# Head of a four-layer graph kernel: unread matmuls while x loads, the first tile by quarters, other orders for the first tiles

## The chip, the cores and the metric

The kernel runs on one core of a Trainium2 chip. The metric is the device time of one execution in microseconds; lower is better. The engines are named as in the profile: PE does matrix products, DVE, ACT and POOL work on vectors, SP issues DMAs.

## What is computed

x has 128 graphs of 64 nodes with 256 features, in float32. Four layers, each with a LayerNorm (without scale) and a ReLU ahead of it, add their result to x. Only the first half of layer 0 is touched here:

```python
h = jnp.maximum(_layernorm(x, axis=-1), 0.0)
h = relu(einsum('ts,bsh->bth', adj, h @ Wg0 + bg0))
h = relu(einsum('ts,bsh->bth', adj, h @ Wg1 + bg1))
# then four LSTMs over windows of 1 to 4 nodes, and x = x + h
# layer 1: graph convolution with two batchnorms; layer 2: three-part graph
# convolution; layer 3: attention within each graph with adj as an added mask
```

## The kernel before, in words

x is seen as 8192 rows of 256 and cut into 16 tiles of 512 rows (`SUP`), each of four quarters (`Q`) of 128 rows: two graphs side by side, so that one 128x128 matrix with adj twice on its diagonal (`adjT_bd`) aggregates both. Tiles are numbered from 0 here.

`graph_part(s)` (from line 427 on) lists the steps of tile s. Each step is put into a list by `at(t, fn, ...)` with a due time, counted from 10 x s (`ROUND`); at the end all steps of all tiles are sorted by due time and called in that order. Nothing else sets the order: each engine executes its instructions in the order in which they were called, and waits on semaphores for what they need. The due times are numbers written by hand, not measured times. The steps of one tile:

- `load` (433): a DMA for x, for tiles 0 and 1 one for each quarter. For tile 0, two quarters are issued by ACT and two by SP.
- `stats` (445): for a quarter, L446 and L447 on DVE, mean and variance.
- `root` (449): L451 on DVE adds eps, L452 on POOL raises to the power -0.5, for several quarters at once.
- `shift` (454): L455 on DVE, minus mean over deviation. `relu` (458): L459 on ACT, one a quarter.
- `aggregate0` (461): L467 on PE, for each half c of the features four 128x128 products of a quarter with `adjT_bd`, into one PSUM bank. `aggregated` (470): L471 on ACT copies the bank to SBUF.
- `weigh` (473): L477 on PE, times Wg0, four 128x256 products for each pair of quarters; `weighed` (480): L483 on DVE adds the bias term `rsb`; `relu1` (486): L488 on ACT.
- the second aggregation, again L467 and L471, a round later.
- `sums` (494): four L498 on POOL, differences of quarters of the matrix. They belong to a product with Wg1 in seven block products instead of eight; `product` (501): L506 on PE, which also needs sums of the blocks of Wg1 (L311 on POOL, from the copies L135). `begun` (509): L513, and `add` (518): L520, on DVE, empty the PSUM banks of the products; a bank is filled by one product, emptied by L513, and filled by the next. `relu2` (535): L536 on ACT.

So a steady round of PE holds seven 128x256 products (L506) of tile s-2, eight 128x128 products (L467) for tile s and eight for tile s-1, and eight 128x256 products (L477). For each tile, DVE calls L455 of a later tile between the L520 and the L513 of an earlier one.

Beside this, POOL prepares the weights of the later LSTMs in the graph part. The constants come first: `first_constants` (adjT), wg0, `second_constants` (adj, bg0), `more_constants` (Wg1 in four copies by L135, and small ones). `row_sums` (155) makes the bias terms from adj (L157, L158) and a product with a matrix of ones (L160, copied by L161). `adjacency_parts` (191) makes four masked forms of adj on POOL (L193 to L202), which SP then stores to DRAM (L203, `parts_d`). Behind it in SP's queue stand the loads of the weights for layer 1 (`load_raw_w1`, L626, into `wc`) and for the LSTM of windows of two (`staging`, L362, into `wb`); POOL adds blocks of them (L311, L369, L384, L389) at due times set by `stage`. L632 stores the sums in `wc` to DRAM (`w_d` in the profile), and after that L369 uses `wc` for the next sums.

Buffers: x has three (`pax`), the other tiles of the graph part two, the LayerNorm's small ones three; PSUM has eight banks, given out in turn by `bank()`.

Of the kernel before, what the change touches and what calls it, by code (L numbers as in the profile page):

```python
# [9 lines left out]
F32 = mybir.dt.float32  # L10
# [4 lines left out]
P = 128  # L15
# [5 lines left out]
def kernel(ctx: ExitStack, tc: tile.TileContext, a: dict, out: bass.AP):  # L21
# [4 lines left out]
    nc = tc.nc  # L26
# [4 lines left out]
    KC = D // P  # L31
    SUP = 512
    NS = NT // SUP
    Q = SUP // P
# [27 lines left out]
    def other_end(name, bufs):  # L62
        scope = ExitStack()
        return scope, scope.enter_context(tc.tile_pool(name=name, bufs=bufs, side="right"))
# [3 lines left out]
    graph_weights, first = other_end("first", 1)  # L68
# [13 lines left out]
    def bank(pool="psum"):  # L82
        return pool() if callable(pool) else banks[pool][1].tile([P, 512], F32, tag="ps", name="ps")
# [4 lines left out]
    def load_const(name, src, shape, pool=const, queue=nc.sync):  # L88
        t = pool.tile(shape, F32, tag=name, name=name)
        queue.dma_start(t, src)  # L90
        return t
# [5 lines left out]
    def weight(name, src, pool=const, queue=nc.sync):  # L97
        k, m = src.shape
        return load_const(name, src.rearrange("(c p) m -> p c m", p=P), [P, k // P, m], pool, queue)

    ident = const.tile([P, P], F32, tag="ident", name="ident")
    make_identity(nc, ident)
    ones = first.tile([P, P], F32, tag="ones", name="ones")
    nc.gpsimd.memset(ones, 1.0)
    mhalf = const.tile([P, 8], F32, tag="mhalf", name="mhalf")
    nc.gpsimd.memset(mhalf, -0.5)
    mone = const.tile([P, Q], F32, tag="mone", name="mone")
# [4 lines left out]
    adjT_bd, adj_bd = (first.tile([P, P], F32, tag=n, name=n) for n in ("adjT_bd", "adj_bd"))  # L112
# [36 lines left out]
    rs_row = first.tile([P, P], F32, tag="rs_row", name="rs_row")  # L149
# [5 lines left out]
    def row_sums():  # L155

        nc.vector.reduce_sum(rs_col, adj_bd, axis=AX.X)  # L157
        nc.vector.tensor_scalar_mul(rsb, con["bg0"], rs_col)  # L158
        ps = bank()
        nc.tensor.matmul(ps[:, :P], ones, adjT_bd, start=True, stop=True)  # L160
        nc.vector.tensor_copy(rs_row, ps[:, :P])  # L161

    def adjacencies():

# [258 lines left out]
    ROUND, HALF = 10.0, SUP // 2  # L423
    with tc.tile_pool(name="pa", bufs=2) as pa, tc.tile_pool(name="pax", bufs=3) as pax:
        events, wih0, made = [], [], []

        def graph_part(s):
            t0, v = ROUND * s, {}

            def at(t, fn, *args):  # L430
                events.append((t0 + t, len(events), fn, args))
# [35 lines left out]
                    nc.tensor.matmul(p_[:, ts(q, P)], v[h][:, q, ts(c, P)], adjT_bd,  # L467
                                     start=True, stop=True)

            def aggregated(g, c):  # L470
                nc.scalar.copy(v[g][:, c, :], v["p", g, c])  # L471

            def weigh(k):
                p_ = v["W", k] = bank().rearrange("p (q d) -> p q d", q=2)
# [67 lines left out]
                at(-10.5, second_constants)  # L542
                at(-20, lambda: con.update(wg0=weight("wg0", a["Wg0"], first)))
            if s == 0:
                halves = ((slice(0, 2), -9.1), (slice(2, 4), -7.4))
                at(-10, new_norm)
                for q in range(Q):
                    at(-9.8 + 0.6 * q, stats, q)
            else:
                halves = ((slice(0, 4), -11.9),)  # L550
                at(-15.2, new_norm)
                for q in range(Q):
                    at((-15.1, -14.5, -13.1, -12.5)[q], stats, q)
            for qs, t in halves:
                at(t, root, qs)
                at(t + (1.4 if s < 2 else 3.0), shift, qs)
                for q in range(qs.start, qs.stop):
                    at((2.7 - ROUND if s == 1 else t + (1.5 if s == 0 else 3.1)) + 0.6 * (q - qs.start), relu, q)
            late, end = 0, s == NS - 1
            for c in range(KC):  # L560
                at(late + 0.86 + 1.75 * c, aggregate0, "g0", "h", c)
                at(late + 0.87 + 1.75 * c, aggregated, "g0", c)
            for k in range(2):
                at(late + 6.56 + 1.72 * k, weigh, k)
                at(late + 8.3 + 1.75 * k, weighed, k)
                at(late + 8.9 + 1.75 * k, relu1, k)
            late += ROUND
            for c in range(KC):
                t = (0.86, 2.6)[c] if end else 4.35 + 0.89 * c
                at(late + t, aggregate0, "g1", "h1", c)  # L570
                at(late + t + 0.01, aggregated, "g1", c)
# [19 lines left out]
            at(late + 7.1, relu2, 1)  # L591

            if s == 0:
                at(2, row_sums)
            if s == 1:
                at(-5, adjacency_parts)
            if s == 2:
# [13 lines left out]
        for s in range(NS):  # L611
            graph_part(s)
# [327 lines left out]
    def first_step(t0, st, tags, names):  # L940

        p, N = st["p"], st["N"]
        input_ = input_sums(st, 0)
        for k in (-9, -8.5, 0.2, 0.4) if st["new"] else (*((-0.8, -0.6) if p == NL else (-3.4, -1.4)), 2.6, 6.6):
            at(t0 + k, next, input_)
        g, end, t = {}, {}, t0
        for (name, gi, fn), tag in zip((g for g in GATES if g[0] != "f"), tags):
            g[name], end[name] = gate(t, st, p - 1, gi, fn, tag, names)
            t += 7
        e = end["g"]  # L950
        cell = cells[st["s"]]

        def start(n):
            i, g_ = (gates[g[k]["tag"]][:, n, :, :N] for k in "ig")
            nc.gpsimd.tensor_mul(cell[:, n, :, :N], i, g_)  # L955

        def squash(n):
            nc.scalar.activation(gates[g["g"]["tag"]][:, n, :, :N], cell[:, n, :, :N], AF.Tanh)

        h_at = t + 13.3  # L960
        for n in range(2):
            at(e + 2.2 + 0.1 * n, start, n)
            at(e + (6.07, 9)[n], squash, n)
            at(h_at + 0.8 * n, state, st, n, g["o"], g["g"], p == 1)
        st["h_at"] = h_at + 0.8
        return t
# [284 lines left out]
    t, tags = 0.0, [0, 1, 2, 3, 4]  # L1251
    plan(t, 2, (2, load_r), *((11 + 3 * k, fetch, name) for k, name in enumerate(("W1", "S1", "S2"))),
         (8, fetch_x), (20, fetch_w2), (25, fetch, "S4"), (28, fetch_s3, 0))
    for p in range(1, NL + 1):
        pairs = pairs_of(p)
        for k in range(0, len(pairs), 2):
# [3 lines left out]
            for i, st in enumerate(sts):  # L1260
                if p == 1:
                    t = first_step(t, st, [tags[(3 * (k + i) + n) % 5] for n in range(3)], FIRST_BANKS)
                else:
# [4 lines left out]
                    t = first_step(t, st, tags[:3] if i == 0 else [*tags[3:], tags[0]], GROUP_BANKS)  # L1268
# [7 lines left out]
            for j in range(1, p):  # L1276
                for st in sts:
# [5 lines left out]
                    t = outer_step(t, st, j, now, fin)  # L1283
                    tags = [now[n] for n in ("spare", "12", "22", "11", "21")]
                    now = dict(zip(("22", "11", "21", "12", "spare"), tags))
            if end and p < NL:
                q = p + 1
# [124 lines left out]
    with tc.tile_pool(name="pz", bufs=1, reuse_waits="tile") as pz:  # L1412
# [248 lines left out]
        late = ctx.enter_context(tc.tile_pool(name="late", bufs=1, side="right", reuse_waits="tile"))  # L1661
# [473 lines left out]
```

## Time and profile before

| | us |
|---|---|
| median of 4 runs (1817.31 to 1818.14) | 1817.99 |
| the profiled execution | 1818.14 |
| its span, from the first instruction to the last | 1816.40 |
| PE busy | 1793.9 (99%) |
| DVE, POOL, ACT busy | 1259.6, 1248.9, 926.9 |
| DMA packets' share of the 16 engines, first queue | 15.3% |

The profile's page gives busy times; its views answer for a stretch of the span. In the timeline each row has the start, the duration, the engine, the line, the operation, what it writes and reads, and xN where N records are merged into one row; in brackets stands the idle time of the engine just before it, with what ended it. A float32 matmul leaves two records. The waits view gives for each engine and line what it waited for: the sum, the number of times, the longest. An engine's name with a q (SPq) is its queue, which issues DMAs. The DMA view gives the time from issue to landing. DMA records and semaphore updates are in the trace too.

### The profile page before, as it was taken

To read this page: it belongs to the slowest core of one execution; us is meant where nothing else is said; L and a number is where in the kernel's file an instruction comes from. 1 tells how busy PE (TensorE), PEld (TensorE's weight loads), DVE (VectorE), ACT (ScalarE), POOL (GpSimd) and SP (SyncE) were. 2 spreads that over 40 slices of the span, in tenths; PEclk is the share of its full clock that TensorE was granted. 3 is DMA by queue.
4 is the path that set the end of the run, shared out by engine and by line. 5 is a ranking of instruction groups with operands and counts; after the bars stand their busy time and mean duration, and the time that the engine had idled before them with its cause. 6 is when DMAs were issued, how large, how long until landed. Compare 5 with 4: busy or idle time off the path is not lost.

```text
span 1816.4 us, 25209 instructions
## 1 busy us (share of the span) xinstructions
PE 1793.9 (99%) x8904; PEld 1330.5 (73%) x8904; DVE 1259.6 (69%) x2462; ACT 926.9 (51%) x1612; POOL 1248.9 (69%) x1275
## 2 busy tenths in 40 slices
PE   8999999999999999999999999999999999999998
PEld 7997444576576888788577776666444899999997
DVE  6875555676666787777677777687876666666675
ACT  6775666633534434434633333577675444444542
POOL 6988454767776777787768887777363666666663
PEclk9999999999999999999999999999999999999999
DMA  6753300000004000001200000333100110111111
GB/s 188 240 189 134 126 1 0 1 1 1 0 1 135 1 1 1 1 1 40 96 0 1 0 1 23 128 120 127 61 1 15 33 48 30 42 47 48 47 36 36
DMA packets 73868, 90.92 MB, mean 50 GB/s; under 512 B 5264, under 2 KB 64528, under 8 KB 73744
## 3 DMA queue, kind: packets, MB, share of 16 engines
q1 hardware_dynamic: 73296, 89.03, 15.3%
q8 instruction: 71, 1.16, 0.3%
q14 instruction: 53, 0.43, 0.1%
q10 hardware_dynamic: 448, 0.30, 0.1%
HBM read 56.01 MB, written 33.29 MB: 49 GB/s over the span
## 4 chain that ended last, share of the span: by engine, by line
PE 57%; DVE 1%; ACT 1%; issue 0%; POOL 0%; DVEq 0%; POOLq 0%; ACTq 0%
PE ps L1080 14%; PE ps L1846 8%; PE ps L1107 7%; PE ps L1323 5%; PE ps L1573 5%; PE ps L1813 3%; PE ps L1917 3%; PE ps L1914 3%; PE ps L908 2%; PE ps L736 2%; PE ps L1953 2%; PE ps L1984 1%; PE ps L689 1%; PE ps L1881 1%; PE ps L1757 1%; PE ps L1857 1%
## 5 line engine op out<-in xcount | busy, mean ns | idle before, releaser
L1092 DVE TENSOR_TENSOR gate<-gate,ps 128x512 f32<-128x512 f32 (+2 forms) x544 | 321.6, 602 | 165.0 <-PE ps L1080 148.4
L1126 ACT ACTIVATE gate<-gate,lbias 128x512 f32<-128x512 f32 (+2 forms) x284 | 173.2, 650 | 326.0 <-DVE gate L1120 312.1
L921 DVE TENSOR_TENSOR gate<-gate,ps 128x512 f32<-128x512 f32 (+2 forms) x162 | 100.5, 642 | 126.9 <-PE ps L908 118.8
L1140 POOL TENSOR_TENSOR cell<-cell,gate 128x1024 f32<-128x1024 f32 (+2 forms) x36 | 73.0, 2029 | 112.5 <-ACT gate L1126 112.5
L1107 PE MATMUL ps<-tx,wb 128*128 128x512 f32 (+2 forms) x320 | 143.5, 537 | 0.0
L1789 ACT ACTIVATE h<-x,ln_rn 128x256 f32<-128x256 f32 x128 | 66.5, 590 | 98.4 <-POOL ln_rn L1786 96.8
L917 ACT ACTIVATE gate<-gate,lbias 128x512 f32<-128x512 f32 (+2 forms) x108 | 95.8, 887 | 34.2 <-DVE gate L921 34.2
L908 PE MATMUL ps<-tx,wih 128*128 128x512 f32 (+2 forms) x252 | 110.5, 554 | 0.2 <-ACT gate L924 0.2
L1846 PE MATMUL ps<-wl,ag 128*128 128x128 f32 x900 | 108.4, 276 | 0.8 <-DVE x L1874 0.2
L1846 PEld LDWEIGHTS ps<-wl,ag 128*128 128x128 f32 x900 | 104.2, 192 | 3.7 <-issue 2.9
L873 POOL TENSOR_TENSOR tx<-hT 128x512 f32<-128x512 f32 (+2 forms) x29 | 36.0, 1242 | 77.3 <-PE ps L908 75.3
L924 ACT COPY gate<-ps 128x512 f32<-128x512 f32 (+2 forms) x108 | 59.4, 550 | 55.7 <-PE ps L908 55.1
L908 PEld LDWEIGHTS ps<-tx,wih 128*128 128x128 f32 x252 | 48.1, 192 | 50.5 <-issue 40.5
L1120 DVE TENSOR_TENSOR gate<-gate,ps 128x512 f32<-128x512 f32 (+2 forms) x136 | 79.0, 598 | 5.4 <-PE ps L1107 3.4
L908 PE MATMUL ps<-hT,wih 128*128 128x512 f32 (+2 forms) x168 | 79.1, 576 | 0.4 <-DVE h L513 0.4
L1137 POOL TENSOR_TENSOR gate<-gate 128x1024 f32<-128x1024 f32 (+3 forms) x37 | 74.3, 2007 | 6.6 <-ACT gate L1126 6.6
L955 POOL TENSOR_TENSOR cell<-gate 128x1024 f32<-128x1024 f32 (+2 forms) x36 | 78.1, 2191 | 0.0
L1080 PEld LDWEIGHTS ps<-h,wb 128*128 128x128 f32 x328 | 58.9, 190 | 23.3 <-issue 11.7
L1143 POOL TENSOR_TENSOR cell<-cell,gate 128x1024 f32<-128x1024 f32 (+3 forms) x37 | 73.2, 1979 | 2.8
L1080 PE MATMUL ps<-h,wb 128*128 128x256 f32 (+2 forms) x328 | 74.9, 351 | 0.0
L1065 POOL TENSOR_TENSOR wih<-wih 128x256 f32<-128x256 f32 (+2 forms) x88 | 67.8, 779 | 7.7 <-DVE wih L1158 5.5
L1923 ACT COPY qh<-ps 128x512 f32<-128x512 f32 x60 | 35.1, 585 | 70.8 <-PE ps L1917 59.3
(359 smaller groups left out, 4968.9 us busy)
## 6 DMA issues: line engine op xcount, KB each, us to landing
xt<-in_x_dram SPq DMA_DIRECT2D x30, 512.0 KB, 4.6
x1d<-xt SPq DMA_DIRECT2D x16, 512.0 KB, 2.9
x<-x1d SPq DMA_DIRECT2D x16, 512.0 KB, 4.5
out_dram<-x SPq DMA_DIRECT2D x15, 512.0 KB, 3.2
wb<-in_WhhT_dram SPq DMA_DIRECT2D x36, 128.0 KB, 4.4
wb<-in_WihT_dram SPq DMA_DIRECT2D x31, 128.0 KB, 3.4
S<-wc SPq DMA_DIRECT2D x3, 896.0 KB, 4.6
W<-wb SPq DMA_DIRECT2D x3, 896.0 KB, 4.9
```

Of the source, the lines that this page charges most:

```text
L908: nc.tensor.matmul(wide(p_[:, :N]), wih_of(p, k, gi), x_, start=first_, stop=True, skip_group_check=True)
L917: nc.scalar.activation(to, r[bank_][:, :N] if bank_ else to, fn, bias=lbias[:, l, m : m + 1])
L921: nc.vector.tensor_add(slot(n, hc), slot(n, hc), r[bank_][:, :N])
L955: nc.gpsimd.tensor_mul(cell[:, n, :, :N], i, g_)
L1080: nc.tensor.matmul(halves_of(to) if pr == 1 else to, w, d, start=(new and g == 0), stop=(name, k) in (("a", 4), ("b", 3), ("c", 2)), skip_ ...
L1092: nc.vector.tensor_add(to, base, v)
L1107: nc.tensor.matmul(to, w, d, start=new, stop=(c == 1), skip_group_check=True)
L1120: nc.vector.tensor_add(part("22" if pr == 7 else "21", k), part("12" if pr == 7 else "21", k), v)
L1126: nc.scalar.activation(v, B[CHAIN.index((hc, g))][:, :N] if fin and m == "21" else v, FN[r, g], bias=lbias[:, l, b : b + 1])
L1323: nc.tensor.matmul(r[name], con["w1"][:, OF[j], g, :], x_, start=new, stop=(name, j) in (("a", 4), ("b", 3), ("c", 2)), skip_group_check=True)
L1573: nc.tensor.matmul(banks[name], w2[:, OF[j], k, :], x_, start=(new and k == 0), stop=(k == 1), skip_group_check=True)
L1846: nc.tensor.matmul(v["g", name][:, p_, :], x_[:, m, ts(p_, P)], wl2[:, OF[j], m, :], start=new and p_ == m == 0, stop=m == 2 and (name, j) ...
```

## The change

It does the following.

1. `ones` is set first on POOL, ahead of the identity matrix.
2. A new step `busy` puts matmuls whose result nobody reads on PE: five of `ones` with `ones` (128x128), then two of `ones` with the first quarter of x (128x256) and one of 128 columns of it, all into one bank.
3. Tile 0: `root`, `shift` and `relu` run quarter by quarter instead of half by half, in the order that the due times give. A new step `aggregate_row` does the first aggregation by quarters, both halves of the features for each (L486 in the changed kernel), into two banks. The two copies go to ACT and to DVE. `weigh`, `weighed` and `relu1` of tile 0 are due right after.
4. Tile 1: its statistics, `root`, `shift` and `relu` run in two halves, with earlier due times.
5. Tile 2: `shift` and `relu` have later due times. The other tiles are as before.
6. `row_sums` is due earlier, and its last copy (L161) is a step by itself.

On PE the order is: the eight unread matmuls, the eight of `aggregate_row`, L160, and from there that of before. POOL has six L452 instead of three ahead of the copies of Wg1. On DVE the statistics of tile 2 stand behind both `weighed` steps of tile 0 (L499 in the changed kernel) instead of ahead of them. SP issues the same DMAs in the same order; the load of tile 3 waits for PE's last unread matmul in place of DVE's last statistics of tile 0. Lines shift: L477 becomes L493, L483 L499, L498 L514, L506 L522, L513 L529, L520 L536, L632 L671.

```diff
+    ones = first.tile([P, P], F32, tag="ones", name="ones")
+    nc.gpsimd.memset(ones, 1.0)
     ident = const.tile([P, P], F32, tag="ident", name="ident")
     make_identity(nc, ident)
-    ones = first.tile([P, P], F32, tag="ones", name="ones")
-    nc.gpsimd.memset(ones, 1.0)
...
-        nc.vector.tensor_copy(rs_row, ps[:, :P])
+        return lambda: nc.vector.tensor_copy(rs_row, ps[:, :P])
...
-            def aggregated(g, c):
-                nc.scalar.copy(v[g][:, c, :], v["p", g, c])
+            def aggregated(g, c, copy=nc.scalar.copy):
+                copy(v[g][:, c, :], v["p", g, c])
+
+            def busy(src, n):
+                if "busy" not in v:
+                    v["busy"] = bank()
+                rhs = src()
+                for _ in range(n):
+                    nc.tensor.matmul(v["busy"][:, : rhs.shape[-1]], ones, rhs, start=True, stop=True)
+
+            def aggregate_row(q):
+                if q == 0:
+                    v["g0"] = pa.tile([P, KC, SUP], F32, tag="g0", name="g0")
+                    for c in range(KC):
+                        v["p", "g0", c] = bank()
+                for c in range(KC):
+                    nc.tensor.matmul(v["p", "g0", c][:, ts(q, P)], v["h"][:, q, ts(c, P)], adjT_bd,
+                                     start=True, stop=True)
...
-                halves = ((slice(0, 2), -9.1), (slice(2, 4), -7.4))
+                halves = ()
                 at(-10, new_norm)
-                for q in range(Q):
-                    at(-9.8 + 0.6 * q, stats, q)
+                at(-20.6, busy, lambda: ones, 5)
+                at(-9.9, busy, lambda: v["xt"][:, 0, :], 2)
+                at(-9.9, busy, lambda: v["xt"][:, 0, :P], 1)
+                for q, t in enumerate((-9.8, -9.6, -9.4, -9.2)):
+                    one = slice(q, q + 1)
+                    at(t, stats, q)
+                    at(t + (0.05 if q < 2 else 0.12), root, one)
+                    at((-9.5, -9.3, -9.1, -8.8)[q], shift, one)
+                    at(-7.6 + 0.6 * q, relu, q)
+            elif s == 1:
+                halves = ()
+                at(-19, new_norm)
+                for q, t in enumerate((-18.7, -18.65, -14.8, -14.7)):
+                    at(t, stats, q)
+                for qs, t, t_shift in ((slice(0, 2), -18.6, -14.9), (slice(2, 4), -14.6, -14.42)):
+                    at(t, root, qs)
+                    at(t_shift, shift, qs)
+                    for q in range(qs.start, qs.stop):
+                        at(t_shift + 0.005, relu, q)
...
-                at(t + (1.4 if s < 2 else 3.0), shift, qs)
+                at(t + (7.35 if s == 2 else 3.0), shift, qs)
                 for q in range(qs.start, qs.stop):
-                    at((2.7 - ROUND if s == 1 else t + (1.5 if s == 0 else 3.1)) + 0.6 * (q - qs.start), relu, q)
+                    at(t + (7.45 + 0.02 * q if s == 2 else 3.1 + 0.6 * q), relu, q)
             late, end = 0, s == NS - 1
-            for c in range(KC):
+            if s == 0:
+                for q in range(Q):
+                    at(-7.5 + 0.6 * q, aggregate_row, q)
+                at(-5.0, aggregated, "g0", 0)
+                at(-5.0, aggregated, "g0", 1, nc.vector.tensor_copy)
+            for c in range(KC) if s else ():
...
-                at(late + 6.56 + 1.72 * k, weigh, k)
-                at(late + 8.3 + 1.75 * k, weighed, k)
-                at(late + 8.9 + 1.75 * k, relu1, k)
+                at(-4.45 + 0.1 * k if s == 0 else 6.56 + 1.72 * k, weigh, k)
+                at(-4.4 + 0.1 * k if s == 0 else 8.3 + 1.75 * k, weighed, k)
+                at(-4.39 + 0.1 * k if s == 0 else 8.9 + 1.75 * k, relu1, k)
...
-                at(2, row_sums)
+                at(-4.5, lambda: v.update(rs=row_sums()))
+                at(-4.2, lambda: v["rs"]())
```

## The prediction

> **What bounds the kernel now.** I read the page first, then the waits of PE, then the timeline of the first 47 us, then its DMA view. All durations come from the profiled execution: 1818.14 us, of which 1816.40 are its span and 1.74 lie around it; the median of the four runs shown is 1817.99, 0.15 lower. The page gives PE 99% busy, and of the 22 us in which it is not, PE's waits put 6.9 in one piece: before its first matmul.
>
> ```profile
> PE 1793.9 (99%) x8904; PEld 1330.5 (73%) x8904; DVE 1259.6 (69%) x2462; ACT 926.9 (51%) x1612; POOL 1248.9 (69%) x1275
> ```
> ```profile
> PE ps L467 <- ACT ln_h L459: 6.9, 1, 6.9
> ```
>
> So the head is PE's alone: it starts at 6.86, reaches the first product of the steady rounds (L506) at 22.47, and then a round takes 10.04 us (products start at 22.47, 32.52, 42.56). Rows of the timeline, start and duration in us, a float32 matmul leaving two records:
>
> ```profile
> 6.86 2.43 PE L467 MATMUL ps<-adjT_bd,ln_h 128*128 128x128 f32 x8 [6.86 <-ACT ln_h L459]
> ...
> 9.50 1.91 PE L467 MATMUL ps<-adjT_bd,ln_h 128*128 128x128 f32 x8
> ...
> 11.21 4.26 PE L477 MATMUL ps<-wg,g 128*128 128x256 f32 x16
> ...
> 12.47 1.00 POOL L135 COPY wg<-wg1p 128x128 f32<-128x128 f32 x4 [1.73 <-DMA wg1p<-in_Wg_dram]
> ...
> 14.86 0.33 SPq L203 DMA_DIRECT2D parts_d<-parts  x1
> ...
> 15.31 1.95 PE L467 MATMUL ps<-adjT_bd,ln_h 128*128 128x128 f32 x16
> ...
> 22.47 1.03 PE L506 MATMUL ps<-g,wg 128*128 128x256 f32 x4
> ...
> 28.92 0.45 SPq L632 DMA_DIRECT2D w_d<-wc  x1
> ```
>
> Two things are to be seen. **The clock:** four 128-wide matmuls (x8) take 1.91 us at 9.50 but 1.05 us at 45.18 (below), so PE runs at half rate at first; its passes double their pace at about 12.3 us. Cold, a 128-wide matmul costs 0.43 us, warm 0.223 (1.78 us from the row at 15.31 to the next eight at 17.09); a 256-wide one 0.86 and 0.43. **A second chain beside PE:** POOL copies wg1 when its DMA lands at 12.4 (issue 7.04, 5.4 to landing), makes the adjacency parts, SP can then issue parts_d at 14.86, and behind that in SP's queue stand twenty weight loads, two tiles of x and the store of wc at 28.92, which lands 6.2 us later. The next rows show where that chain meets PE.
>
> ```profile
> 35.26 2.56 POOL L369 TENSOR_TENSOR wc<-wb 128x512 f32<-128x512 f32 x2 [1.42 <-DMA w_d<-wc]
> ...
> 43.92 1.00 POOL L452 TENSOR_TENSOR ln_rn<-ln_rn,mhalf 128x4 f32<-128x4 f32 x1
> ...
> 44.91 2.09 POOL L384 TENSOR_TENSOR wb<-wb 128x256 f32<-128x256 f32 x3
> 44.96 0.69 DVE L455 SCALAR_TENSOR_TENSOR ln_rn<-ln_mv,ln_rn 128x4 f32<-128x4 f32 x1 [0.59 <-POOL ln_rn L452]
> ...
> 45.18 1.05 PE L467 MATMUL ps<-adjT_bd,ln_h 128*128 128x128 f32 x8
> 45.57 0.86 DVE L513 SCALAR_TENSOR_TENSOR h<-rs_row,bg,ps 128x256 f32<-128x256 f32 x2
> ...
> 46.09 0.70 PE L506 MATMUL ps<-g,wg 128*128 128x256 f32 x2
> ```
>
> POOL sat idle 1.42 us until the store landed at 35.1, because L369 overwrites wc. From there POOL is busy without a break up to tile 4's rsqrt (L452, ending 44.93); DVE stands at tile 4's shift (L455) for it, then empties the bank (L513, first of two, over at 46.04), and PE's L506 starts at 46.09. PE by itself would have been ready at 45.18 + 4 x 0.223 = 46.07. **The two chains arrive within 0.02 us of each other.** The store's landing is set by DMAs, not by PE.
>
> **The change part by part.**
>
> *Unread matmuls.* Five 128-wide on ones (from about 1.3, when POOL's now first memset is through) and, once x's first quarter has landed at 3.5, two 256-wide and one 128-wide: cold 5 x 0.43 and 2 x 0.86 + 0.43, ending near 3.5 and 5.85. They lie in PE's 6.86 us of idleness and end before the first relu; if they ended later, each 0.1 us would delay the first tile by as much. They free nothing by themselves; they bring the warm clock earlier. When is not shown, so both ends: warm at 5.5, or not before 12.3 as now. I take 8.9, one clock window of 3.41 us (the length of the half-rate stretch at 578.9) before today's 12.3.
>
> The trace rates PE busy 2.0 of 3.4 us in the stretch up to 8.9, which was not enough, and fully busy in the next, which was. [...]
>
> *First tile by quarters.* Quarter 0: stats 3.51 to 4.15 (L446 0.43, L447 0.18), L451 to 4.4, a one-column pow on POOL. The trace has none: two columns take 0.71, four 1.01, a memset of four 0.10; between 0.10 and 0.71 I take 0.56, by the slope of the two rows. Then shift, and relu 5.3 to 5.9 (L459, 0.59). DVE runs in order and each shift waits for its pow, so later quarters follow every 0.75 to 0.9 us: relus end at 5.9, 6.6, 7.5, 8.4. The last is no earlier than today's (8.44). PE's eight matmuls begin at 5.95 instead of 6.86 and end at about 9.2 (8 cold). The two copies now run side by side on ACT (0.585) and DVE (not in the trace; the DVE add from the same bank takes 0.68, ACT's copy 0.585; I take 0.62): both done by 10.0, against 11.46 + 0.58 = 12.04. The first weigh matmuls start at 9.8 and 10.25, instead of 11.21 and 12.09. Eight x 0.43 end at 13.26; the next row of PE now begins at 15.31: **2.05 us gained**. The row sums matmul (0.22 to 0.43) fills the wait for the copies.
>
> *Second tile (tile 1) in halves.* Its relus end at 13.4 (POOL's second two-column pow 11.4 to 12.1, shift, two relus), needed at 13.9; cover 0.5. Relu1 of tile 0 ends at 14.0 and 14.8, needed at 15.05 and 15.5. rsb needs bg0 (issue 5.93, landing 4.3 us later), done at 11.9, used at 12.2. Then 1.79 + 1.79 + 3.44 of matmuls: first product at 20.3 instead of 22.47, **2.2 us ahead** (2.5 with warm at 5.5, 1.0 with 12.3).
>
> *What moves behind it.* DVE now does tile 2's statistics after tile 0's sums, at 14.3 instead of 11.68, so POOL's pow for tile 2 goes from 14.91 to 16.9, and all that stands behind it on POOL follows: four L311 (1.81), four L498 (2.9), tile 3's pow (1.01), to 23.5 (24.2 now). DVE waits for that at L455, and behind L455 stand the evacuations: L455 0.69, L513 0.47, and PE's third product pair, due at 23.8 by then, at 24.65. **0.85 is lost, 1.4 stays** (1.7 and 0.1 at the two clock ends). SP's order is unchanged. Tile 3's load now also waits for the last unread matmul (5.9), but stood until 10.3 for bg0's landing anyway. The pows in front of wg1's copies on POOL end at 12.1 (12.3 cold), wg1 lands at 12.4: cover 0.1 to 0.3.
>
> *The sum.* So wg1's copies, parts_d at 14.86, the loads, the store, L369 at 35.26, L452 at 44.93 and L513 at 46.04 all keep their times. PE comes to its L506 at 44.7 instead of 46.07, and **waits 1.4 us for the same bank**. Of the head's 2.2 us, 0.85 is lost at 24 and the rest at 46; 0 to 0.2 remain (0.2: added up in this way row by row, today's own starts in this stretch come out within that). 1818.14 - 0.15 = 1818.0 on the profiled execution's scale, 1817.8 on the median's.
>
> L455's duration decides 0.5 of that: 0.16 where POOL is idle (34.24), 0.69 where a POOL op starts just ahead (44.91). [...]
>
> **Rivals.**
> 1. *The meeting point gives way.* [...] Against: the waits at L369 and L455 are real and nothing in front of them moves; and at 148.28 PE waits 0.96 us for the same L513, behind a POOL that waited for DMA, which would eat 1.0 of a larger gain. All 1.4 kept gives 1816.4; 0.5 kept 1817.3. Chance 0.22.
> 2. *The clock warms late*, slower than before: unread matmuls stop, PE stands in short gaps between quarters, and the warm clock comes after 12.3. That is the point from which it decides: at 14.0 the third pair is 0.7 us late and stays so past 46, at 15.7 1.6: 1818.7 to 1819.6. Against: from 5.95 cold matmuls of 0.43 arrive faster than they run. Chance 0.07.
> 3. *POOL's second pow for tile 1* slips past 12.4 and pushes wg1's copies and the whole DMA chain one for one: +0.1 to 0.5, 1818.0 to 1818.4. Chance 0.06.
> 4. *The half-rate window at 578.9* (clock 0.51 in that window; passes of 0.53 us where 0.27 is usual, six of them: 1.6 us), which follows a PE wait of 2.0, falls elsewhere: 1816.2 without it. Chance 0.04.
>
> **The numbers.** Forecast 0.61: 1817.3 to 1818.3, best 1817.8. The range takes in most of rival 1 (from 1816.3) and the mild half of 2 and all of 3 (to 1818.8); about 0.14 stays out. 0.2% is 3.6 us, about what a measurement of this kernel can tell from no change; the head's whole gain is 2.5 at most, so faster by that much needs rivals 1 and 4 together and more: 0.02. Slower needs twice the dearest case of 2: 0.01. Same: 0.97.
>
> **What would show it.** PE's first L486 near 5.95; the first L493 near 9.8, the first L522 near 20.3; a PE wait on L529 near 24.6; L369 at 35.2 after a longer POOL wait (2.8 instead of 1.42) ended by the store; PE idle some 1.2 to 1.5 us before L522 at 46.1. Wrong, if wg1's copies or parts_d start at another time, if L369 starts over 0.3 us earlier, or if PE's L522 runs through 46 without a wait.

## The result and the profile after

The changed kernel takes 1820.22 us (median of 33 runs), the kernel before 1818.17 (53 runs beside it): ratio 1.0010, interval 1.0005 to 1.0015, 0.9 to 2.7 us slower. Forecast were 1817.8 and a range up to 1818.8. The profiled execution took 1820.18 us. Its page:

```profile
span 1818.4 us, 25254 instructions
...
PE 1797.5 (99%) x8920; PEld 1332.4 (73%) x8920; DVE 1262.3 (69%) x2469; ACT 926.5 (51%) x1611; POOL 1250.3 (69%) x1278
```

PE is again 99% busy. Of its waits, two lines tell the story: 1.1 us stand before the first matmul instead of 6.9, and 3.5 us for DVE's L529 have come (1.0 for the same thing, then L513, before).

```profile
PE ps L522 <- DVE h L529: 3.5, 4, 1.9
...
PE ps L478 <- POOL ones L102: 1.1, 1, 1.1
```

The head does what it was forecast to do. The timeline's rows of PE (start, duration, then engine and line):

```profile
3.45 2.30 PE L478 MATMUL ps<-xt,ones 128*128 128x256 f32 x6
...
6.06 1.17 PE L486 MATMUL ps<-adjT_bd,ln_h 128*128 128x128 f32 x8 [0.30 <-DMA adjT_bd<-in_adjT_dram]
...
9.47 3.72 PE L493 MATMUL ps<-wg,g 128*128 128x256 f32 x16 [0.23 <-ACT g L471]
...
20.05 1.03 PE L522 MATMUL ps<-g,wg 128*128 128x256 f32 x4
...
24.41 0.70 PE L522 MATMUL ps<-g,wg 128*128 128x256 f32 x2 [0.49 <-DVE h L529]
```

The first product comes 2.42 us earlier (22.47 before); 1.45 are left from the third pair on. The other chain, SP's DMAs and POOL, in the same timeline:

```profile
15.16 0.33 SPq L203 DMA_DIRECT2D parts_d<-parts  x1
...
20.86 3.23 SPq L362 DMA_DIRECT2D wb<-in_WhhT_dram  x4
...
30.00 0.45 SPq L671 DMA_DIRECT2D w_d<-wc  x1
...
36.59 2.56 POOL L369 TENSOR_TENSOR wc<-wb 128x512 f32<-128x512 f32 x2 [4.20 <-DMA w_d<-wc]
...
45.24 1.02 POOL L452 TENSOR_TENSOR ln_rn<-ln_rn,mhalf 128x4 f32<-128x4 f32 x1
...
46.30 0.68 DVE L455 SCALAR_TENSOR_TENSOR ln_rn<-ln_mv,ln_rn 128x4 f32<-128x4 f32 x1 [3.38 <-POOL ln_rn L452]
...
47.42 0.70 PE L522 MATMUL ps<-g,wg 128*128 128x256 f32 x2 [1.85 <-DVE h L529]
```

Everything here is later than in the profile of before: parts_d by 0.30, the store by 1.08, L369 and all behind it by 1.33. PE comes early, waits 1.85 us and starts 1.33 us later than before (46.09). A second loss of 1.0 us stands at 97, where the profile of before shows nothing. The changed kernel, then the same places in the one before:

```profile
81.39 5.56 SPq L362 DMA_DIRECT2D wb<-in_WihT_dram  x8
...
89.57 2.57 POOL L369 TENSOR_TENSOR wc<-wb 128x512 f32<-128x512 f32 x2 [0.96 <-DMA wb<-in_WihT_dram]
...
97.15 0.67 PE L522 MATMUL ps<-t,wg 128*128 128x256 f32 x2 [0.52 <-DVE h L536]
```
```profile
80.09 4.45 SPq L362 DMA_DIRECT2D wb<-in_WihT_dram  x8
...
87.24 1.30 POOL L369 TENSOR_TENSOR wc<-wb 128x512 f32<-128x512 f32 x1
...
96.57 0.70 PE L506 MATMUL ps<-g,wg 128*128 128x256 f32 x2
97.11 0.62 PE L506 MATMUL ps<-t,wg 128*128 128x256 f32 x2
```

Before, the same eight loads take SP 4.45 us, the seventh lands at 87.04 and L369 starts at 87.24 without a wait: a cover of some 0.05 us, since L369 follows a landing by 0.15. This execution is a tight one here too: in the five other profiles of the kernel before and its variants in which L369 does not wait, the same cover is 0.40 to 0.66 us. After 98.6 the two kernels keep their distance to the end.

What lies in the loads of WihT is a code fetch, by the name that the DMA view gives its queue (instruction). In the DMA view of the changed kernel, 82 to 84 us (queue, packets, MB, share of the DMA engines' time):

```profile
q8 instruction: 1, 0.02, 3.0%
```

Queue q8 has 71 packets of 16 KB in the whole run, one per 251 of PE's 17,840 instructions (products and weight loads), so I take these to be PE's fetches, and the 54 of 8 KB of q14 those of the other engines; the experiments below bear this out, since PE's instructions moved the ones and DVE's the others. This one starts at 82.70 and takes 0.96 us. Before, the corresponding fetch (the fourth on q8 in either kernel) starts at 88.32 and takes 1.13 us, behind the weight loads. In both kernels the load of tile 10 lands at the head of them; in the changed one the first WhhT behind it lands 1.85 us later (83.17, 85.02), before 0.44 later (82.11, 82.55).

### The profile page after: what moved, and what is told of

Same layout as the page of the kernel before. It is cut to its first block, busy times and chain, and to the rows that moved or that the text cites. A ratio compares the mean times of both kernels' runs of the same rounds, so it can differ in the third digit from the quotient of the medians.

```text
span 1818.4 us, 25254 instructions
## 1 busy us (share of the span) xinstructions
PE 1797.5 (99%) x8920; PEld 1332.4 (73%) x8920; DVE 1262.3 (69%) x2469; ACT 926.5 (51%) x1611; POOL 1250.3 (69%) x1278
## 4 chain that ended last, share of the span: by engine, by line
PE 57%; DVE 1%; ACT 1%; issue 0%; POOL 0%; DVEq 0%; POOLq 0%; ACTq 0%
PE ps L1119 14%; PE ps L1885 8%; PE ps L1146 7%; PE ps L1362 5%; PE ps L1612 5%; PE ps L1852 3%; PE ps L1956 3%; PE ps L1953 3%; PE ps L947 2%; PE ps L775 2%; PE ps L1992 2%; PE ps L2023 1%; PE ps L728 1%; PE ps L1920 1%; PE ps L1796 1%; PE ps L1896 1%
## 5 line engine op out<-in xcount | busy, mean ns | idle before, releaser
L963 ACT COPY gate<-ps 128x512 f32<-128x512 f32 (+2 forms) x108 | 59.4, 550 | 56.6 <-PE ps L947 56.0
```

## The experiments

All figures of PE below are the start of one and the same matmul less its start in the profile shown of before: at 42.6 (what the head has gained), at 46.1 (the third product pair of that round) and at 98.6. The times are medians of 8 to 11 runs, those of the kernel before from 21 to 33 runs on the same chip.

| kernel | at 42.6 | at 46.1 | at 98.6 | median us | before beside | ratio, interval |
|---|---|---|---|---|---|---|
| before_again | -0.32 | +1.33 | +1.35 | 1818.27 | 1818.22 | 0.9992 to 1.0010 |
| before_dvepad | +0.32 | +0.98 | +0.91 | 1818.43 | 1818.22 | 0.9991 to 1.0009 |
| after_dvepad | -1.11 | +1.14 | +1.92 | 1818.51 | 1818.22 | 0.9995 to 1.0013 |
| after_store | -1.46 | -1.02 | +0.17 | 1817.07 | 1818.22 | 0.9983 to 1.0000 |
| after_again | -1.45 | +1.60 | +2.20 | 1819.32 | 1818.58 | 0.9999 to 1.0017 |
| after_no_unread | -0.73 | +0.41 | +0.42 | 1817.97 | 1818.58 | 0.9988 to 1.0006 |
| before_unread | -0.22 | +1.35 | +2.12 | 1818.68 | 1818.58 | 0.9997 to 1.0015 |
| before_store | -0.21 | -0.23 | -0.34 | 1816.38 | 1818.58 | 0.9985 to 1.0003 |
| after_unread4 | -0.60 | +0.84 | +1.60 | 1818.90 | 1818.23 | 0.9995 to 1.0013 |
| both_no_unread | -1.07 | -0.87 | -0.85 | 1816.52 | 1818.23 | 0.9981 to 0.9999 |
| both_x10 | -1.50 | -0.92 | -0.03 | 1816.24 | 1818.23 | 0.9981 to 0.9999 |
| before_store2 | -0.37 | -0.39 | -0.52 | 1816.74 | 1818.23 | 0.9985 to 1.0002 |
| after_x10_early | -1.42 | +1.51 | +1.53 | 1818.20 | 1817.60 | 0.9996 to 1.0014 |
| both_x10_early | -1.58 | -1.07 | -1.06 | 1815.69 | 1817.60 | 0.9981 to 0.9999 |
| after_unread2 | -0.10 | +1.70 | +2.61 | 1819.47 | 1817.60 | 1.0001 to 1.0019 |
| after_unread16 | +1.94 | +3.87 | +4.35 | 1821.81 | 1817.60 | 1.0013 to 1.0033 |
| before_pool3 | -0.18 | +2.14 | +3.72 | 1818.33 | 1818.24 | 0.9993 to 1.0011 |
| both_pool4 | -1.55 | -0.90 | -0.95 | 1815.00 | 1818.24 | 0.9977 to 0.9995 |

The profile shown of the changed kernel has -1.45, +1.33 and +2.34. My theory at the start (A): code fetches, moved by the added instructions, fall into SP's weight loads and delay the DMA and POOL chain. Against it stood chance (B) and the half-rate windows (C).

**before_again**: the kernel before without an edit.

> The kernel before, unchanged, as the measure of chance. Theory A (the added instructions move the code fetches of DVE and PE into the stretches in which SP issues weight loads, and each holds that queue for 1.2 us): the fetches stay where they were in the profile shown of before, DVE's first at 27.9 +- 0.5 us and PE's at 26.7 +- 0.5, the store of wc is issued at 28.9 +- 0.3, PE's third product pair starts at 46.1 +- 0.3; ratio 1.000. Rival B (the lateness of the changed kernel is the chance of one execution): the store's issue scatters by about 1 us from one profile to the next and PE's start at 46 with it. Rival C (the difference is one more half-rate window of 3.4 us, 1.7 us each): these runs list granted clocks of 1.0 more often than the changed kernel's, and runs of equal clock differ by less than 0.5 us from the changed kernel's.

Measured: the store is issued at 30.25, not 28.92, and L369 and PE in its timeline stand where they do in the changed kernel:

```profile
36.59 2.55 POOL L369 TENSOR_TENSOR wc<-wb 128x512 f32<-128x512 f32 x2 [3.06 <-DMA w_d<-wc]
```
```profile
47.42 0.70 PE L506 MATMUL ps<-g,wg 128*128 128x256 f32 x2 [1.51 <-DVE h L513]
```

So B is right at 46: the same kernel starts there 1.33 us apart in two executions, and the profile that I had read is the early one. 0.45 of it stands at parts_d already (15.31 against 14.86), and the first quarter of x on ACT's queue landed at 3.28 there, against 3.58 and 3.60 in before_again and in the changed kernel; that the one causes the other is not shown.

Theory C is not settled by this run. Runs of it that list the same granted clock are 0.38 us (at 1.000) and 0.76 us (at 0.999) below those of the changed kernel by their medians, partly within C's 0.5.

**after_dvepad**, **before_dvepad**: in the changed kernel (22) and in the one before (11).

```diff
+    idle = const.tile([P, 1], F32, tag="idle", name="idle")
+    for _ in range(22):
+        nc.vector.memset(idle, 0.0)
```

> The changed kernel with 22 one-column memsets on DVE in its idle first 3 us: nothing is computed otherwise, but DVE comes to its 65th instruction at about 14.5 us instead of 21.46. Theory A: the fetch of 8 KB moves with it to 14 to 15 us, where SP issues nothing; the gap of 1.7 us between two loads of WhhT goes; the store of wc is issued at 29.2 instead of 30.0, L369 starts about 0.8 us earlier, PE's third product pair at 46.6 instead of 47.4; the time is 0.5 to 1.0 us under the changed kernel's 1820.2, unless PE's fetch at 82.7 takes the same again. Rival B: no change beyond chance, and the gap stays. Rival C: no change.

> The kernel before with 11 one-column memsets on DVE in its idle first 3 us, so that DVE reaches its 65th instruction at about 21.4 us instead of 26 to 27. Theory A: the fetch falls at 21.4 to 22, SP shows a gap of about 1.7 us between two loads of WhhT there, the fetch at 27.93 is gone; the store of wc is issued 0.3 to 0.8 us later than 28.9 and PE's third product pair starts as much later than 46.1: 1818.5 to 1819.0. Rival B and C: 1818.2 as before.

Measured: DVE's fetch moved, from 21.46 and 27.93 to 14.00 (expected 14 to 15) and 20.71 (expected 21.4 to 22), and in after_dvepad SP's gap among the second WhhT loads is gone (3.23 us in the changed kernel):

```profile
21.66 2.04 SPq L365 DMA_DIRECT2D wb<-in_WhhT_dram  x4
```

But the store, issued 1.38 us earlier, lands at 35.97 instead of 36.08: six weight loads and a tile of x, 1.3 MB, are still under way in front of it, and the hole in SP's issue was made good before it landed. Of the 0.8 us expected at 46, 0.19 came. In before_dvepad the fetch took 0.31 us and opened no gap, so that this run doesn't test what a gap costs. No run shows that DVE's fetch costs anything at 46.

**after_store**, **before_store**, and once more **before_store2**:

```diff
-        stage(5, lambda: nc.sync.dma_start(summed["w1"], wcf))
+        events.append((23.95, len(events), lambda: nc.sync.dma_start(summed["w1"], wcf), ()))
```

> The changed kernel with the store of wc issued ahead of the load of tile 5 instead of behind it. Theory A, and with it that this DMA chain and not PE sets the start at 46: the store lands about 2.2 us earlier (33.9), L369 starts at about 34.1 instead of 36.6, PE's third product pair at 44.6 to 45.0 instead of 47.4, and the time falls by 1.5 to 2.5 us, to 1817.7 to 1818.7. If PE or chance sets the time (rivals B and C), it moves by less than 0.5 us.

> The kernel before with the store of wc issued ahead of the load of tile 5. A2: an ordinary execution of it waits 0.9 to 1.3 us at 46 for the store's landing (the profile shown of before, with 0.0, was an early one); with the store 2.2 us earlier PE's third product pair starts at 45.8 to 46.1 on its own, and the time falls by 0.7 to 1.2 us, to 1817.0 to 1817.5. Rival (the profile of before is the rule: PE and the chain meet at 46 within 0.02 us): 1818.2, no change.

> The kernel before with the early store once more, beside the three others: 1.0 to 2.0 us under the kernel before, PE's third product pair at 45.8 to 46.1. It is the mark for what the head's change adds once the store no longer decides at 46.

Measured in after_store, POOL and PE:

```profile
34.23 2.56 POOL L369 TENSOR_TENSOR wc<-wb 128x512 f32<-128x512 f32 x2 [1.84 <-DMA w_d<-wc]
```
```profile
45.07 0.70 PE L522 MATMUL ps<-g,wg 128*128 128x256 f32 x2 [0.29 <-DVE h L529]
```

L369 is 2.36 us earlier and PE 2.35. In before_store PE runs through 46 without a wait (45.87); in before_store and before_store2 the medians are 2.2 and 1.5 us below the kernel before, though their intervals end at 1.0003 and 1.0002. The store's landing, not PE, sets the start at 46 in ordinary executions of both kernels, and the head's gain is lost there. At 98.6 after_store loses 1.19 us again; before_store nothing.

**after_again** (no edit), **after_no_unread** (the three lines with busy taken out), **before_unread** (the function busy and these lines put into the kernel before):

```diff
+                at(-20.6, busy, lambda: ones, 5)
+                at(-9.9, busy, lambda: v["xt"][:, 0, :], 2)
+                at(-9.9, busy, lambda: v["xt"][:, 0, :P], 1)
```

> The changed kernel, unchanged, beside the three others. Theory A now has two parts. A1: PE's code fetch at 82.7 us (88 to 89 in the kernel before) opens a gap of 1.85 us in SP's loads of WihT, POOL's L369 waits 1.0 us for the last of them at 88.6, and PE loses 1.0 us at 97: this is there in every execution of the changed kernel and in none of the kernel before. A2: at 46 both kernels wait for the store of wc, whose landing scatters by about 1.3 us between executions of either; the 1.45 us that PE is ahead by then are lost there whichever comes. So: the gap at 83 and POOL's wait of 1.0 again, the store issued at 28.6 to 30.3, PE's third product pair at 47.1 to 47.5, and 1.0 to 2.0 us over the kernel before. Rival B (chance): the gap at 83 is absent or elsewhere.

> The changed kernel without the unread matmuls, all else kept: 32 instructions fewer on PE. A1: PE's fetch at 82.7 moves 2 to 6 us later, to 85 to 89, out of the loads of WihT; the gap of 1.85 us at 83 goes, L369 doesn't wait at 88.6, PE loses nothing at 97: 1.0 us under the changed kernel in the same session, although PE's clock is warm only at 8 to 12 us and PE reaches the first product 0.5 to 1.5 us later, which the wait at 46 swallows. Rival D (the unread matmuls are what the head gains by): the time rises by 0.5 to 1.5 us.

> The kernel before with the unread matmuls alone: 32 instructions more on PE in a stretch in which it is idle. A1: PE's fetch moves from 88 to 89 to 83 to 86 us; if it falls into the loads of WihT (81 to 86) SP shows a gap of 1.5 to 1.9 us there, POOL's L369 waits 0.5 to 1.0 us, and the time is 0.5 to 1.0 us over the kernel before. Rival D: the earlier clock makes the head 0.5 to 1 us shorter and the time falls, or nothing moves.

Measured: PE's fetch is at 82.58, 88.41 and 82.47; the loss between 85 and 98.6 is 0.60, 0.01 and 0.77. SP and POOL in after_no_unread, then in before_unread:

```profile
80.48 4.06 SPq L362 DMA_DIRECT2D wb<-in_WihT_dram  x8
```
```profile
87.66 2.56 POOL L369 TENSOR_TENSOR wc<-wb 128x512 f32<-128x512 f32 x2
```
```profile
81.42 5.33 SPq L362 DMA_DIRECT2D wb<-in_WihT_dram  x8
```
```profile
89.37 1.30 POOL L369 TENSOR_TENSOR wc<-wb 128x512 f32<-128x512 f32 x1 [0.72 <-DMA wb<-in_WihT_dram]
```

The second loss comes and goes with the unread matmuls alone, in either kernel. Without them the changed kernel is 1.35 us faster, run beside it on the same chip (1817.97 and 1819.32, medians of 11 runs that spread over 4 us), though its head gains only 0.73 us. The time of before_unread is 0.10 us over the kernel before, with an interval of -0.5 to 2.7 us, which neither shows its loss nor excludes it. In the profiles rival D is answered: what the unread matmuls give the head (0.7 us) is lost at 46, and they cost at 97.

after_again is the unedited changed kernel, run beside the kernel before. Runs of the two that list the same granted clock differ by 0.87 us at 1.000 (medians 1818.11 and 1817.24) and by 1.14 at 0.999 (1820.07 and 1818.93). So C, which allowed less than 0.5, isn't the whole; the groups are small (4 to 19 runs).

**after_unread4**, **after_unread2**: four or two of the matmuls on ones, none on x. **after_unread16**: `at(-20.6, busy, lambda: ones[:, :1], 13)` in place of the five.

```diff
-                at(-20.6, busy, lambda: ones, 5)
-                at(-9.9, busy, lambda: v["xt"][:, 0, :], 2)
-                at(-9.9, busy, lambda: v["xt"][:, 0, :P], 1)
+                at(-20.6, busy, lambda: ones, 4)
```

> The changed kernel with four of its eight unread matmuls (the four on ones): half the dose, 16 instructions fewer on PE. A1: PE's fetch falls between 82.6 (eight) and 88.4 (none), at 84 to 87 us; the loads of WihT are issued by 85.6, so most or all of the gap at 83 goes, L369 waits 0 to 0.5 us and PE loses 0 to 0.4 us at 97 instead of 0.6 to 1.0. Rival E (it is the work of the unread matmuls, or the warm clock, that costs, and not where the fetch falls): the loss at 97 halves with the number of matmuls, to about 0.4, with the gap still at 82 to 83.

> The changed kernel with two of its eight unread matmuls, 24 instructions fewer on PE. With four the fetch stood at 82.35, as with eight (82.6), with none at 88.4: it doesn't move in proportion. If it is tied to a fixed place in PE's stream that the sequencer reaches where it isn't held up by a wait, there is a number at which it jumps: with two it stands at 82 to 83 with a loss of 0.6 to 1.0 at 97, or at 86 to 89 with none, and not between. If it goes by count, 86 to 87.

> The changed kernel with sixteen unread matmuls (thirteen of one column, which end as early, instead of the five on ones): 32 instructions more on PE. If the fetch goes by count it falls 2 to 4 us earlier, at 78 to 81, among the loads of WhhT and WihT, which it holds back as much: a loss of 0.5 to 1.0 at 97. If it jumps to 76 or earlier, before those loads are queued, nothing is lost at 97 and the time is 0.6 to 1.0 us under the changed kernel. Rival E: the loss grows with the number of matmuls.

Measured: fetch at 82.35 (four), 83.41 (two) and 81.22 (sixteen); loss 0.77, 0.91 and 0.49. Neither my 84 to 87 for four nor rival E's halving came: from none to two the place jumps by 5 us, from two to eight it hardly moves. after_unread16 says little of the loss: 26 passes of one column took 5.71 us, so that the whole head came 3.4 us late.

**both_no_unread**, **both_x10**: the early store in the changed kernel, once without the unread matmuls, once with tile 10's load behind the weight loads (`-20.95 if s == 10`).

> The changed kernel without the unread matmuls and with the store of wc ahead of the load of tile 5. If A1 and A2 are the whole story, they add: at 46 PE starts on its own at 45.3 to 45.5 (0.73 ahead of the profile shown of before), no gap at 83, nothing lost at 97; 0.4 to 0.6 us under the kernel before with the early store alone, 1.5 to 2.2 under the kernel before. If the store alone is what pays: the same as the kernel before with the early store, within 0.2.

> The changed kernel with its unread matmuls, with the store of wc ahead of the load of tile 5, and with the load of tile 10 (issued at 76 us) behind the weight loads instead of ahead of them. A1: PE's fetch stays at 80 to 81 and the gap in the loads of WihT stays, but the last of them lands about 2 us earlier, so that POOL's L369 does not wait for it; PE keeps its 1.0 us of lead through 97, 1.0 to 1.2 us better than with the early store alone there; 1.8 to 2.5 us under the kernel before. Rival E: the loss of 1.2 at 97 is there as before.

Measured: in the profile the first adds up as expected (nothing lost from 46 to 575). Its time is 1.71 us below the kernel before, but only 0.22 below before_store2 beside it, where 0.4 to 0.6 were expected and the rival said within 0.2: the times do not part the two. In the second PE's fetch came at 78.62, earlier than the 80 to 81 expected, and SP still shows a gap of 1.4 us among the loads of WihT. POOL's L369 doesn't wait any more, yet 0.89 us are lost at 98.6: DVE now waits for tile 10.

```profile
88.27 0.43 DVE L446 BATCH_NORM_STATS2 ln_st<-xt 128x6 f32<-128x256 f32 x1 [1.28 <-DMA xt<-in_x_dram]
```

By itself this would suit E as well, so the load was moved the other way.

**after_x10_early**, **both_x10_early** (with the early store):

```diff
-            at(-21 if s < 3 else -26, load)
+            at(-21 if s < 3 else -28.4 if s == 10 else -26, load)
```

> The changed kernel with the load of tile 10 issued some 8 us earlier, ahead of the store at 77.4 us and so in a stretch in which SP and the DMAs are idle; nothing on PE, DVE, ACT or POOL is touched. A1: PE's fetch stays at 82 to 83 and holds the loads of WihT back as before, but the 512 KB that stood in front of them are gone, so that the last of them lands about 1.5 to 2 us earlier, before POOL comes to L369 at 88.6: no wait there, nothing lost at 97, 0.6 to 1.0 us under the changed kernel. Behind the weight loads, where the load of tile 10 stood in another run, it made DVE's statistics wait; here it lands earlier, so that they don't. Rival E (the loss at 97 comes from the work added on PE): it stays, 0.6 to 1.0.

> The same together with the early store of wc. A1 and A2 together: PE at 46 is 0.9 to 1.0 us ahead of the profile shown of before and keeps that through 97; 0.3 to 0.6 us under the kernel before with the early store, and 1.7 to 2.5 us under the kernel before, the fastest of all. Rival E: 0.9 to 1.2 are lost at 97 as with the early store alone.

Measured: in after_x10_early the fetch is still there (81.29), SP still has a gap, and POOL does not wait:

```profile
81.02 4.77 SPq L362 DMA_DIRECT2D wb<-in_WihT_dram  x8
```
```profile
88.75 2.57 POOL L369 TENSOR_TENSOR wc<-wb 128x512 f32<-128x512 f32 x2
```

Nothing is lost between 46 and 98.6 (+0.02, and +0.01 with the early store), with every unread matmul in place. E falls: the matmuls cost by where the fetch lands and by the thin cover there. The time of after_x10_early can't show its 0.6 to 1.0 us: no unedited changed kernel ran beside it, and it stands 0.6 us over the kernel before, with an interval from -0.7 to 2.5.

**before_pool3**, **both_pool4**: one-column memsets on POOL behind that of eps, three and four.

> The kernel before with three one-column memsets on POOL, which is idle then: its stream is as much longer as in the changed kernel, and nothing else is changed. In the six profiles of kernels with the old POOL stream L369 starts 0.15 to 0.16 us after the store's landing, in the twelve with the new one 0.50 to 0.52, with a pause of 0.48 between POOL's two semaphore events ahead of it. Theory F: POOL's sequencer pauses once at a fixed place of its stream, and three more instructions move that place in front of L369. So the lag is 0.50 to 0.52, and PE starts as much later at 46: 0.3 us over the kernel before, too little for the timed runs to tell. Rival: the lag belongs to what the changed kernel does (its order of semaphores), and stays at 0.16.

> The changed kernel with the early store and the early load of tile 10, and four one-column memsets more on POOL in its idle start. Theory F: the pause now falls ahead of the wait for the store, where POOL is idle anyway; the lag is 0.16 again, L369 starts 0.35 us earlier and PE's third product pair 0.3 to 0.35 earlier, at 1.35 to 1.45 ahead of the profile shown of before, nearly all that the head gains by 42; the time is 0.3 us under the same kernel without them, 1815.4. Rival: the lag stays at 0.51 and the time at 1815.7.

Measured: the lag, from the store's landing to L369, is 0.16 in both. Theory F failed in the first and held in the second: three more instructions alone don't bring the lag of 0.51, four more on top take it away. What ties it to the stream stays open; that it is the same in all profiles of one stream is shown. In both_pool4 the store landed 0.56 us later than in both_x10_early, so that PE gained nothing at 46 in that profile. Its 1815.00 us is the lowest median, 0.9977 to 0.9995 of the kernel before: the early store, the early load of tile 10 and the head together beat the kernel before. How much of its lead over both_x10_early is the lag and how much comes from the runs being made at another time isn't told apart.

The profile of before_pool3 also shows a stretch at half rate right behind a wait of PE of 1.8 us. By windows (length; busy time of PE, PEld, DVE, ACT and POOL with the number of instructions; PEclk, the granted clock; DMA share and GB/s):

```profile
44.90:48.40 3.50, 1.65 (x11) 1.41 (x12) 1.29 (x3) 0.60 (x3) 3.50 (x5) 1.00 0.02 5
48.40:51.80 3.40, 3.40 (x13) 3.03 (x14) 2.10 (x8) 2.02 (x5) 2.83 (x5) 0.50 0.67 228
```

PE was busy for 1.65 us of the first (47%), the second ran at half rate (0.50), and 1.62 us went between 46 and 56.6; that the wait set off the half rate is not shown.

## Why the prediction was wrong, point by point

- **Unread matmuls**: ended at 3.55 and 5.75 (forecast 3.5, 5.85). The clock, by the trace's clock record, was warm at 5.42 (12.31 before), at the early bound of 5.5 and not at 8.9, which was my choice between the two bounds. Right, and too cautious.
- **First tile**: pow of one column 0.55 (0.56); first aggregation at 6.06 (5.95), held by adjT's landing and not by a relu; DVE's copy 0.69 (0.62); weigh at 9.47 (9.8), over at 13.19 (13.26); first product 20.05 (20.3), 2.42 ahead (2.2). Right.
- **Loss of 0.85 at the third pair**: it starts at 24.41 (24.65), held by L529 behind L455 behind POOL's pow; 1.57 are left there, 1.45 a round on (1.4). Right.
- **"wg1's copies, parts_d at 14.86, the loads, the store, L369 at 35.26, L452 at 44.93 and L513 at 46.04 all keep their times"**: this is the step that failed. The mechanism was right: the chain of DMAs and POOL decides at 46, PE waits there (1.85; I had said 1.4), POOL waits for the store (4.20; I had said 2.8), L455 takes 0.68 again (I had 0.69; 0.15 at 32.79, where POOL stands idle, and why it is longer at 46 is not shown), and the head's gain is eaten. But I took the times of one execution for the kernel's. Of the 1.33 us by which L369 is later, 0.98 is the store's landing (36.08 against 35.10), and in before_again, without an edit, the store lands 1.33 later (36.43); the two chains that I saw meet "within 0.02 us" lie 0.7 to 2.3 us apart, PE first, in the four other profiles of before and its variants with the store in its old place. By itself this leaves the two kernels equal, as both wait for the store; what makes the changed one slower are the next two points.
- **A second part of the same step** was never worked out: L369 starts 0.15 to 0.16 us behind the store's landing in all seven profiles of kernels derived from before, 0.50 to 0.52 in the twelve derived from the changed one without added memsets on POOL. This 0.35 is the rest of the 1.33 and comes with the change; its cause stays open.
- **Behind 46** I checked one wait (148.28) and took all else as unmoved. "nothing in front of them moves" was said of what the diff moves. The 32 instructions more on PE moved its fetch from 88 to 82.7, into loads that had 0.05 to 0.66 us of cover, and put these back by more than that: 0.6 to 1.0 us. This is shown in the profiles by taking the matmuls out, putting them into the kernel before, and widening the cover.
- **The rivals**: none was it. Rival 1 gave the meeting point a chance to come earlier, not later; 2 and 3 did not occur (wg1's copies start at 12.77 because wg1 landed 0.30 later, the pows ended at 11.94); the window of rival 4 is at 582 again, but see below.
- **The sum**: 0.35 at 46 and 0.6 to 1.0 at 97 make 0.95 to 1.35 us, within both measurements (0.9 to 2.7 when first measured, -0.2 to 3.1 in after_again). Runs that list the same clock agree with it: they differ by 0.87 and 1.14 in after_again, and in the first measurement by 1.05 at 1.000 (medians 1818.39 of 11 runs, and 1817.34 of 66 runs of before beside the experiments) and by 1.49 at 0.999 (1820.27 of 16, 1818.78 of 84). The rest of the first 2.05 goes with a lower clock: seven of the 34 runs of the changed kernel then list a granted clock of 0.998, with a median of 1822.79; none of the 150 runs of before beside the experiments does (two of 11 in before_unread, one of 11 in after_unread2, none in after_again). A second half-rate window behind the longer wait at 46, as in before_pool3, would do it, but no profile of the changed kernel shows one there, so this part is not shown.

## What to carry to other kernels

Before a gain in front of a meeting point is counted, find which of the two chains waits in ordinary executions: one profile can be an early one by more than the gain. Here a chain of loads with 0.05 to 0.66 us of cover lost it to a code fetch of 0.96 us, and the added instructions moved that fetch far from the edit (from 88.32 to 82.70 us, by matmuls ahead of 6 us). Widen the cover first: here the early store put the kernel before 1.5 and 2.2 us lower by its medians, and the early load of tile 10 took the changed kernel's loss at 97 away. Only then does a shorter head show behind 98.6, and in the profiles alone: 0.5 to 0.7 us in both_x10_early against before_store and before_store2. No timed run shows this part by itself.

## What the runs showed of the hardware

- **With a code fetch among them, data loads landed later.** With a fetch of 16 KB (0.96 us, at 82.70) in the middle of queued loads, the load behind it landed about 1.4 us later than without (1.85 us behind the landing ahead of it, against 0.44). In eight of the nine profiles with the fetch at 80.6 to 83.4, two landings among tile 10 and the loads of WhhT and WihT behind it lie 1.60 to 1.92 us apart (0.91 in after_unread16); in the eight with the fetch at 87 or later no two lie more than 0.85 apart. The cost of the one at 82.70 was not hidden: POOL's L369 waited 0.96 us for a load of WihT, and 1.0 us was lost at 97.
- **The place of PE's fetch did not move in proportion to the instructions added**: 88.4, 83.4, 82.4 and 82.6 to 82.7 us for none, two, four and eight matmuls.
- **The half-rate window came partly by chance**: 11 of the 20 profiles have it, starting at 577.8 to 582.5 us, one has it at 48.4 instead, eight have none; before_store has none and before_store2, the same kernel, has one. Where it is missing PE gains 1.69 us (from +2.05 at 575 to +0.36 at 590 in before_unread). Runs of one kernel spread over 2.2 to 6.0 us. The changes of the clock lie whole multiples of 3.413 us apart: 166, 167 and 528 of them behind 12.31 in the profile of before, 169, 170 and 531 behind 5.42 in that of the changed kernel. In the twelve profiles PE was busy for 43 to 46% of the stretch of that length just ahead of the half rate (1.46 us of 3.41 in these two), and where none followed near 577, for 45 to 69% of the emptiest one there. The two ranges overlap, so what decides is not shown.
- **Unread matmuls of one column were hardly cheaper than wide ones** at the start of the kernel: 26 passes in 5.71 us in after_unread16, 0.22 each, where ten of 128 columns took 2.50 in the changed kernel, 0.25 each. Nor was the clock warm earlier with them: in the nine profiles with all eight unread matmuls as in the changed kernel it was warm at 4.4 to 6.6 us, in the ten with four or fewer at 9.6 to 13.1, in after_unread16 at 12.33.
